# Attention a: outputs and the next keys' and values' parts one round later, the keys' rotation in two parts, weight codes converted in four passes

## The chip, the core and the metric

The kernel runs on one NeuronCore of one Trainium2 chip. A core has five engines that run their own instruction streams and meet only at semaphores: TensorE (PE; its weight loads are listed apart as PEld), VectorE (DVE), ScalarE (ACT), GpSimd (POOL) and SyncE (SP), which here issues the DMAs. Work that is being multiplied or accumulated sits in PSUM, everything else in SBUF. The metric is the device time of one execution in microseconds; smaller is better. Three runs of the kernel before took 1109.16, 1109.80 and 1110.39 us, median 1109.8 us.

## The reference, cut to what matters

The program is four layers on x of shape (2, 512, 512), each added to x after a layer norm: attention a, a mixture of low-rank experts, attention b, and the experts again. All the changed lines are in attention a:

```python
def _dequant(codes, scales):                       # codes 0..15, one scale per 128 rows and column
    return (codes.astype(jnp.float32) - 8.0) * jnp.repeat(scales, 128, axis=0)

q = h @ _dequant(q_codes, q_scales)                # h (2, 512, 512), q: 32 heads of 128
k = h @ _dequant(k_codes, k_scales)                # 8 heads of 128
v = h @ _dequant(v_codes, v_scales)
q, k = _rope(q), _rope(k)                          # pairs turned by position
k, v = jnp.repeat(k, 4, axis=1), jnp.repeat(v, 4, axis=1)
scores = jnp.einsum('bhqd,bhkd->bhqk', q, k) * 128**-0.5 + causal_mask
out = jnp.einsum('bhqk,bhkd->bhqd', jax.nn.softmax(scores), v)
return out.reshape(2, 512, 4096) @ _dequant(o_codes, o_scales)
```

## The kernel before

**Tiles.** Attention a is 64 units: 8 key heads g, 2 batches b, and 4 query heads h of each key head. A unit is one 128-wide head over 512 positions. Activations are kept transposed (head dimension on the partitions, positions along the free side) and are split into a high and a low part in a reduced-precision fp32 type, xh and xl, so that a projection is two matmuls of 128 x 512 into one PSUM bank. The scale of a group of 128 rows can only be applied to a finished 128-row product, so each projection is four products c = 0..3, each of a high and a low matmul (L358, L359). Product 0 is taken out of PSUM by ACT (L363), products 1 to 3 are multiplied by their scale and added by DVE (L365).

**The stages of a unit.** `rotated` projects and turns a query or key head: four products, two DVE multiplies of 64 partitions that swap the halves (L374, L375), then a POOL multiply and a POOL add (L376, L377). `softmaxed` makes four score tiles of 128, 256, 384 and 512 columns (i = 0..3): matmul (L396), a DVE reduction that adds the mask and finds the maximum (L399), ACT exponential (L404), after every second tile a DVE reciprocal (L411) and two POOL multiplies (L413). `weighted` transposes the probabilities on PE (L424), copies them out on ACT (L425), multiplies them by v in eight short matmuls (`av`, L429), and splits the result into ah (ACT, L151) and al (DVE, L152). `output` multiplies ah and al by the head's part of the output weight, n = 0..3 (L438, L439); product 0 goes through ACT into `part` (L445) and POOL adds it to the accumulator (L446), products 1 to 3 are multiplied and added by DVE (L448). `keys_values` projects the next key head's keys and values for both batches; values are transposed on PE (L385).

**Periods and rounds.** The loop over n starts one unit per period and runs five stages of different units side by side: `weighted` of unit n-3, `rotated` of unit n, `output` of unit n-4, `softmaxed` of unit n-2, and some parts of `keys_values`. The stages are generators; `in_turn` takes one step from each in that order, which makes a round. So in round i the program lists: the transposes of tile i, query product i, output product i, score tile i, and one key or value product. A tile scheduler then orders each engine's instructions: the earlier an instruction is in the program, the higher its priority, and an instruction that the scheduler believes not to be ready is passed by a later one. The engines run the resulting order strictly, each instruction waiting at the head of its engine's queue. In the order that results, PE places query product i behind the transposes of tile i and, where the output's operands are there in time, the two matmuls of output product i next to each other.

**Buffers that matter.** PSUM has eight banks: two each for projections (`ps_mm`), outputs (`ps_o`), scores (`ps_sc`), and transposes together with `av` (`ps_tp`). So query product c waits for the evacuation of the product two before it, and output product n for that of product n-2.

**Weights.** Codes arrive by DMA as 128 x 2048 int32 tiles; ACT subtracts 8 and writes the fp32 weight in one instruction (L317), 18 times in all: query and output weights of each g, and the second half of the key and value weights. POOL converts the first half of the key and value weights.

```python
            turn.append(some(more, 3 + (units[min(n, 63)][0] == 0)))
```

This line gives the key and value work three steps per period, four in the first eight periods. From n = 60 on, the first expert layer of batch 0 (`early`) begins beside the last units; what follows attention a is the same code before and after.

Of the kernel before, what the change touches and what calls it, by code (L numbers as in the profile page):

```python
# [14 lines left out]
AF = mybir.ActivationFunctionType  # L15
# [7 lines left out]
NC = DM // P  # L23
# [4 lines left out]
U = 512  # L28
# [12 lines left out]
def kernel(  # L41
# [21 lines left out]
    nc = tc.nc  # L63
# [216 lines left out]
    with ExitStack() as actx:  # L280
# [27 lines left out]
        def whole(codes, u, what, pool=wpool, gpsimd=False):  # L308

            cd = big.tile([P, NC * U], I32, tag="big", name=f"codes_{what}_{u}")  # L310
            nc.sync.dma_start(cd, codes[u])
            w = pool.tile([P, NC, U], F32R, tag="w", name=f"w_{what}_{u}")
            wf = w.rearrange("p c n -> p (c n)")
            if gpsimd:
                nc.gpsimd.tensor_scalar(wf, cd, -8.0, 1.0, ALU.add, ALU.mult)
            else:
                nc.scalar.activation(wf, cd, AF.Copy, bias=-8.0)  # L317
            return w

        wkv, xh, xl, own = {}, {}, {}, {}  # L320
# [2 lines left out]

        own["k"] = own_scales(k_scales, 2 * 4 * NC, "k")
        wkv["k"] = whole(k_codes, 0, "k", wkvp, gpsimd=True)
        own["q"] = own_scales(q_scales, 8 * 4 * NC, "q")
        wq = {0: whole(q_codes, 0, "q")}
        load_x("a", 1, ptp, "pT")

# [12 lines left out]
        nc.sync.dma_start(tab, rope_a)  # L342
        own["v"] = own_scales(v_scales, 2 * 4 * NC, "v")
        wkv["v"] = whole(v_codes, 0, "v", wkvp, gpsimd=True)
        two_parts(1)

# [6 lines left out]
        def projected(kind, w, u, h, b, nm):  # L353

            r = rp.tile([P, S], F32, tag=f"r{kind}", name=f"r_{nm}")
            for c in range(NC):
                ps = ps_mm.tile([P, S], F32, tag="mm", name=f"ps_{nm}_{c}")
                nc.tensor.matmul(ps, w[:, c, ts(h, A_HD)], xh[b][:, c, :], start=True, stop=False)  # L358
                nc.tensor.matmul(ps, w[:, c, ts(h, A_HD)], xl[b][:, c, :], start=False, stop=True)  # L359
                n = (u * NC + c) * 4 + h  # L360
                s = own[kind][:, n : n + 1]
                if c == 0:
                    nc.scalar.activation(r, ps, AF.Copy, scale=s)  # L363
                else:
                    nc.vector.scalar_tensor_tensor(r, ps, s, r, ALU.mult, ALU.add)  # L365
                yield
            return r

        def rotated(dst, kind, w, u, h, b, nm):


            r = yield from projected(kind, w, u, h, b, nm)
            rs = rp.tile([P, S], F32, tag=f"rs{kind}", name=f"rs_{nm}")
            nc.vector.tensor_tensor(rs[0:64], r[64:128], tab[64:128, 1, :], ALU.mult)  # L374
            nc.vector.tensor_tensor(rs[64:128], r[0:64], tab[0:64, 1, :], ALU.mult)  # L375
            nc.gpsimd.tensor_tensor(r, r, tab[:, 0, :], ALU.mult)  # L376
            nc.gpsimd.tensor_tensor(dst, r, rs, ALU.add)  # L377
            yield
# [54 lines left out]
            yield  # L433

        def output(w, h, head, b, ah, al, nm):
            for n in range(NC):
                ps = ps_o.tile([P, S], F32, tag="o", name=f"ps_o_{nm}_{n}")
                nc.tensor.matmul(ps, w[:, h, ts(n, P)], ah, start=True, stop=False)  # L438
                nc.tensor.matmul(ps, w[:, h, ts(n, P)], al, start=False, stop=True)  # L439
                s, to = so[:, head * NC + n : head * NC + n + 1], acc[b][:, n, :]  # L440
                if head == 0:
                    nc.scalar.activation(to, ps, AF.Copy, scale=s)
                elif n == 0:
                    part = rp.tile([P, S], F32, tag="part", name=f"part_{nm}")
                    nc.scalar.activation(part, ps, AF.Copy, scale=s)  # L445
                    nc.gpsimd.tensor_tensor(to, to, part, ALU.add)  # L446
                else:
                    nc.vector.scalar_tensor_tensor(to, ps, s, to, ALU.mult, ALU.add)  # L448
                yield

        def in_turn(*stages):
            stages = list(stages)
            while stages:
                stages = [st for st in stages if next(st, stages) is not stages]
# [21 lines left out]
        def keys_values(g):  # L476

            u, h = divmod(g, 4)
            if g == 4:
                wkv["k"] = whole(k_codes, u, "k", wkvp)  # L480
                wkv["v"] = whole(v_codes, u, "v", wkvp)
            for b in range(B):
                kTs[g, b] = kvp.tile([P, S], F32, tag="kT", name=f"kT_{g}_{b}")
                vs[g, b] = kvp.tile([P, NT, P], F32, tag="v", name=f"v_{g}_{b}")
                yield from rotated(kTs[g, b], "k", wkv["k"], u, h, b, f"k_{g}_{b}")
                yield from values_of(vs[g, b], wkv["v"], u, h, b, f"v_{g}_{b}")

        def chain(*stages):
            for stage in stages:
                yield from stage  # L490

        def some(stage, n):
            for _ in range(n):
                next(stage, None)
                yield


        more = keys_values(0)
        in_turn(some(more, 5))
        units = [(g, b, h) for g in range(A_NKV) for b in range(B) for h in range(A_G)]  # L500
        wo, qTs, prs, ats = {}, {}, {}, {}
        for n in range(len(units) + 4):
# [13 lines left out]
            if at(0):  # L516
                g, b, h, nm = at(0)
                if (b, h) == (0, 0):
                    if g:
                        wq[g] = whole(q_codes, g, "q")  # L520
                    wo[g] = whole(o_codes, g, "o")
                    after = keys_values(g + 1) if g + 1 < A_NKV else iter(())
                    more = chain(more, after)
                qTs[g, b, h] = qtp.tile([P, S], F32, tag="qT", name=f"qT_{nm}")
                turn.append(rotated(qTs[g, b, h], "q", wq[g], g, h, b, f"q_{nm}"))
            if at(4):
                g, b, h, nm = at(4)
                turn.append(output(wo[g], h, g * A_G + h, b, *ats.pop((g, b, h)), nm))
            if at(2):
                g, b, h, nm = at(2)  # L530
                prs[g, b, h] = []
                turn.append(softmaxed(prs[g, b, h], qTs.pop((g, b, h)), kTs[g, b], nm))
            turn.append(some(more, 3 + (units[min(n, 63)][0] == 0)))
            if n == 60:

# [531 lines left out]
```

## Time and profile before

| | |
|---|---|
| median of three runs | 1109.8 us |
| the profiled execution's own time | 1109.65 us |
| its span | 1107.9 us |
| PE busy | 1058.2 us, 96% |
| PE weight loads busy | 709.3 us, 64% |
| DVE busy | 862.7 us, 78% |
| ACT busy | 616.9 us, 56% |
| POOL busy | 586.3 us, 53% |
| first `av` matmul of attention a | 60.3 us |
| weight conversion on ACT, 128 x 2048 | 1.91 us each, 18 of them |

The span is cut into 40 slices on the page; attention a fills the first 25 of them, up to about 700 us. A group of instructions is given with its busy time, the mean duration of one, and the idle time of its engine just before it with what ended that idle time. Matmuls are pipelined: a matmul's duration covers its weight's wait and its latency, so that two neighbours overlap and PE looks busy even where the next one starts late. The distance from the start of one matmul to the start of the next, read in the timeline, shows that; it is called the pitch below.

### The profile page before, as it was taken

The numbers are of one execution on the slowest core, as the hardware profiler recorded it, in microseconds if no ns is written. First come the engines' busy times: TensorE is split into PE (matmuls) and PEld (weight loads), VectorE is DVE, ScalarE is ACT, GpSimd is POOL, SyncE is SP. The second block draws the span as 40 slices with busy tenths as digits, with TensorE's granted clock in tenths as the row PEclk, the third lists the DMA queues.
The fourth block names the chain that finished last, engine by engine and source line by source line (L and its number), as shares of the span: only waits on it lengthen the run. The fifth ranks groups of instructions, "written<-read, shape, count | busy, mean of one in ns | idle before, by whom it ended". The sixth has DMA issues, their size and how long they took to land.

```text
span 1107.9 us, 16182 instructions
## 1 busy us (share of the span) xinstructions
PE 1058.2 (96%) x4940; PEld 709.3 (64%) x4940; DVE 862.7 (78%) x2175; ACT 616.9 (56%) x1421; POOL 586.3 (53%) x916
## 2 busy tenths in 40 slices
PE   4799999999999999999999999999989999999988
PEld 3467777777777677777677777556457555565534
DVE  6889899999999999999999888665386677766142
ACT  3566665566656656665666666523156577675410
POOL 2466556656656556566666666353235576544200
PEclk9899999999999999999999999999999999989999
DMA  7300010121110110110112000023352235211010
GB/s 290 114 1 32 8 39 1 39 76 39 38 39 1 39 39 1 38 39 1 39 45 70 1 1 1 1 94 91 99 178 57 80 107 165 90 39 45 18 48 38
DMA packets 23270, 60.47 MB, mean 55 GB/s; under 512 B 4368, under 2 KB 5328, under 8 KB 20368
## 3 DMA queue, kind: packets, MB, share of 16 engines
q1 hardware_dynamic: 23184, 59.44, 16.4%
q8 instruction: 40, 0.66, 0.2%
q14 instruction: 46, 0.38, 0.1%
HBM read 45.53 MB, written 12.85 MB: 53 GB/s over the span
## 4 chain that ended last, share of the span: by engine, by line
PE 83%; DVE 6%; DMA 3%; POOL 3%; ACT 2%; issue 2%; SPq 0%; ACTq 0%; DVEq 0%; POOLq 0%
PE av L429 12%; PE sc L396 12%; PE tp L424 6%; PE ps_o L438 5%; PE ps_o L439 5%; PE ps_q L358 5%; PE ps_q L359 5%; PE ph_f L207 5%; PE py_f L266 4%; PE num_b L831 3%; PE st_b L805 3%; PE sc_b L758 3%; PE po L887 2%; PE pq_b L678 2%; DMA spread_q<-hl 1%
## 5 line engine op out<-in xcount | busy, mean ns | idle before, releaser
L404 ACT ACTIVATE p<-sc,nmx 128x128 f32<-128x128 f32 (+3 forms) x256 | 135.5, 529 | 95.6 <-DVE nmx L399 92.7
L376 POOL TENSOR_TENSOR r_q<-r_q,tab 128x512 f32<-128x512 f32 x64 | 82.4, 1287 | 191.4 <-DVE rs_q L375 191.4
L396 PE MATMUL sc<-kT,qT 128*128 128x128 f32 (+3 forms) x512 | 180.2, 433 | 0.7 <-POOL qT L377 0.7
L365 DVE SCALAR_TENSOR_TENSOR r_q<-ps_q,s_q,r_q 128x512 f32<-128x512 f32 x192 | 143.6, 748 | 37.2 <-PE ps_q L359 23.3
L413 POOL TENSOR_SCALAR p<-p,rden 128x128 f32<-128x128 f32 (+3 forms) x256 | 139.6, 558 | 59.2 <-DVE rden L411 20.5
L425 ACT COPY pT<-tp 128x128 f32<-128x128 f32 (+3 forms) x256 | 109.3, 427 | 104.3 <-PE tp L424 103.6
L762 DVE CUSTOM_DVE_ANT_0 sc_b<-sc_b,tri 128x128 f32<-128x128 f32 (+3 forms) x256 | 119.7, 517 | 49.5 <-PE sc_b L758 40.4
L429 PE MATMUL av<-pT,v 128*128 128x512 f32 (+3 forms) x512 | 148.5, 433 | 0.0
L429 PEld LDWEIGHTS av<-pT,v 128*128 128x128 f32 x512 | 97.0, 190 | 80.2 <-issue 53.9
L448 DVE SCALAR_TENSOR_TENSOR acc<-ps_o,s_o,acc 128x512 f32<-128x512 f32 x186 | 137.5, 739 | 5.5 <-PE ps_o L439 5.4
L399 DVE CUSTOM_DVE_ANT_0 sc<-sc,tri 128x128 f32<-128x128 f32 (+3 forms) x256 | 125.4, 490 | 7.9 <-PE sc L396 7.0
L358 PE MATMUL ps_q<-xh,w_q 128*128 128x512 f32 x256 | 123.8, 483 | 7.8 <-DVE r_q L365 7.8
L424 PE MATMUL tp<-ident,p 128*128 128x128 f32 x640 | 112.9, 272 | 2.4 <-POOL p L413 2.4
L396 PEld LDWEIGHTS sc<-kT,qT 128*128 128x128 f32 x512 | 95.9, 189 | 24.7 <-ACT p L404 1.5
L811 ACT ACTIVATE pT_b<-st_b 128x384 f32<-128x384 f32 (+1 forms) x192 | 90.5, 528 | 35.6 <-PE st_b L805 34.4
L438 PE MATMUL ps_o<-ah,w_o 128*128 128x512 f32 x256 | 108.0, 422 | 1.7 <-DVE acc L448 1.0
L439 PE MATMUL ps_o<-al,w_o 128*128 128x512 f32 x256 | 104.8, 410 | 3.5 <-DVE al L152 3.5
L424 PEld LDWEIGHTS tp<-ident,p 128*128 128x128 f32 x640 | 82.9, 141 | 30.4 <-issue 6.4
L359 PE MATMUL ps_q<-xl,w_q 128*128 128x512 f32 x256 | 102.2, 399 | 0.0
L814 POOL TENSOR_SCALAR_AFFINE_SELECT pT_b<-pT_b 128x128 f32<-128x128 f32 (+1 forms) x192 | 63.0, 338 | 65.2 <-ACT pT_b L811 62.0
L377 POOL TENSOR_TENSOR qT<-r_q,rs_q 128x512 f32<-128x512 f32 x64 | 85.3, 1334 | 1.0
L446 POOL TENSOR_TENSOR acc<-acc,part 128x512 f32<-128x512 f32 x62 | 79.7, 1285 | 10.1 <-ACT part L445 10.1
(179 smaller groups left out, 2042.5 us busy)
## 6 DMA issues: line engine op xcount, KB each, us to landing
codes_q<-in_q_codes_dram SPq DMA_DIRECT2D x8, 1024.0 KB
codes_o<-in_o_codes_dram SPq DMA_DIRECT2D x8, 1024.0 KB
spread_q<-hl SPq DMA_DIRECT2D x16, 512.0 KB
qs<-spread_q SPq DMA_DIRECT2D x32, 256.0 KB
x_a<-in_x_dram SPq DMA_DIRECT2D x8, 256.0 KB
codes_k<-in_k_codes_dram SPq DMA_DIRECT2D x2, 1024.0 KB
codes_v<-in_v_codes_dram SPq DMA_DIRECT2D x2, 1024.0 KB
x_r<-in_x_dram SPq DMA_DIRECT2D x8, 256.0 KB
```

The lines of the kernel that those rows point to most:

```text
L358: nc.tensor.matmul(ps, w[:, c, ts(h, A_HD)], xh[b][:, c, :], start=True, stop=False)
L359: nc.tensor.matmul(ps, w[:, c, ts(h, A_HD)], xl[b][:, c, :], start=False, stop=True)
L365: nc.vector.scalar_tensor_tensor(r, ps, s, r, ALU.mult, ALU.add)
L396: nc.tensor.matmul(sc[:, :n], qT[:, ts(i, P)], kT[:, :n], start=True, stop=True)
L399: nc.vector.tensor_tensor_reduce(sc[:, :n], sc[:, :n], tri[:, S - n :], -(A_HD**-0.5), 3e38, ALU.add, ALU.min, nmx,)
L404: nc.scalar.activation(pr, sc[:, :n], AF.Exp, bias=nmx, scale=-1.0, accum_out=den[:, i % 2 : i % 2 + 1],)
L413: nc.gpsimd.tensor_scalar(prs[j], prs[j], rden[:, j % 2 : j % 2 + 1], 1.0, ALU.mult, ALU.mult)
L424: nc.tensor.transpose(tp[:, j, :], prs[i][:, ts(j, P)], ident)
L429: nc.tensor.matmul(av[:, j * P :], v[:, j, :], pT[:, j, j * P :], start=(j == 0), stop=(j == NT - 1))
L438: nc.tensor.matmul(ps, w[:, h, ts(n, P)], ah, start=True, stop=False)
L439: nc.tensor.matmul(ps, w[:, h, ts(n, P)], al, start=False, stop=True)
L448: nc.vector.scalar_tensor_tensor(to, ps, s, to, ALU.mult, ALU.add)
```

## The change

Four edits, all in attention a:

- `output` begins with a bare step, so its product n stands in round n+1; the last one falls in a round of its own, with the key and value parts.
- `some` begins with a bare step as well, so the key and value parts take rounds 1 to 3 (1 to 4 in the first eight periods) where they took rounds 0 to 2 (0 to 3). The call ahead of the loop takes six steps in place of five.
- In `rotated`, keys (not queries) get a step between the two DVE multiplies that swap the halves. A key head now has six steps instead of five.
- The conversion of codes on ACT is four instructions of 128 x 512 in place of one of 128 x 2048.

```diff
             else:
-                nc.scalar.activation(wf, cd, AF.Copy, bias=-8.0)
+                for c in range(NC):
+                    nc.scalar.activation(wf[:, ts(c, U)], cd[:, ts(c, U)], AF.Copy, bias=-8.0)
             return w
...
             nc.vector.tensor_tensor(rs[0:64], r[64:128], tab[64:128, 1, :], ALU.mult)
+            if kind == "k":
+                yield
             nc.vector.tensor_tensor(rs[64:128], r[0:64], tab[0:64, 1, :], ALU.mult)
...
         def output(w, h, head, b, ah, al, nm):
+
+            yield
             for n in range(NC):
...
         def some(stage, n):
+            yield
             for _ in range(n):
                 next(stage, None)
                 yield
...
         more = keys_values(0)
-        in_turn(some(more, 5))
+        in_turn(some(more, 6))
```

No matmul, transfer or buffer is added or taken away. ACT has 54 more instructions (72 conversions in place of 18). The order of the instructions that SP issues is the same as before; on PE, DVE, ACT and POOL the order changes throughout attention a and is the same again from the norm of the first expert layer on batch 1 on.

## The prediction

> **What bounds the kernel now.** I read the page first, then busy time by stage, then the chain that ended last, then the waits of PE, then the timeline of two periods. The page shows PE full through the whole of attention a, which is the first 25 slices, and DVE nearly so:
>
> ```profile
> span 1107.9 us, 16182 instructions
> PE 1058.2 (96%) x4940; PEld 709.3 (64%) x4940; DVE 862.7 (78%) x2175; ACT 616.9 (56%) x1421; POOL 586.3 (53%) x916
> PE   4799999999999999999999999999989999999988
> DVE  6889899999999999999999888665386677766142
> ```
>
> Busy time in three stretches, each cut where an `av` begins (columns: length, then busy time of PE, PEld, DVE, ACT, POOL, granted clock, DMA share, GB/s): eight periods with key and value work, the next four, and eight without it.
>
> ```profile
> 488.65:572.98 84.33, 83.30 (x377) 60.78 (x376) 77.38 (x169) 51.57 (x129) 52.61 (x60) 1.00 0.08 26
> 572.98:614.01 41.03, 40.70 (x185) 29.64 (x184) 38.14 (x84) 24.94 (x63) 26.27 (x30) 1.00 0.24 78
> 614.01:688.94 74.93, 74.93 (x338) 54.47 (x337) 65.44 (x153) 45.87 (x120) 46.47 (x56) 1.00 0.00 1
> ```
>
> PE is busy 74.93 of 74.93 us, and yet not at its pace. In the timeline a matmul over 512 columns is followed by the next after 0.23 us, a transpose after 0.108, and the score and `av` matmuls come as two records each, 0.108, 0.215, 0.322 and 0.428 apart by width. A unit without keys and values has 16 wide matmuls, 10 transposes and eight record pairs: 3.68 + 1.08 + 2 x 2.146 = 9.05 us. It takes 74.93/8 = 9.37. Adding 0.23 for each key or value matmul and 0.43 for a transposed value tile, I set each `av`-to-`av` distance against its own contents. From 60.3 to 698.4 us, 61 periods take 638.1 us for 609.0 us of pitches: 29.1 us are hidden waits. The starts in the chain show where they lie:
>
> ```profile
> 488.81 2.16 PE av L429 x8
> 499.09 2.16 PE av L429 x8
> 510.40 2.16 PE av L429 x8
> 520.52 2.16 PE av L429 x8
> 529.84 2.16 PE av L429 x8
> 540.60 2.16 PE av L429 x8
> 548.08 1.07 DVE rs_k L375
> 551.82 2.16 PE av L429 x8
> ```
>
> By these contents most periods lose 0.17 to 0.32 us, the one from 499.09 loses 0.89, the one from 540.60 loses 1.25. The waits that PE and its weight loads show from 60 to 700 us name the two causes, and the timeline the events:
>
> ```profile
> PEld ps_o L439 <- DVE al L152: 9.1, 20, 1.8
> PEld ps_q L358 <- DVE r_q L365: 7.2, 7, 1.0
> ```
>
> ```profile
> 501.59 1.13 DVE L374 TENSOR_TENSOR rs_q<-r_q,tab 64x512 f32<-64x512 f32 x1
> 502.75 0.69 DVE L152 TENSOR_TENSOR al<-av,ah 128x512 fp32r<-128x512 f32 x1
> 503.50 0.19 PEld L439 LDWEIGHTS ps_o<-al,w_o 128*128 128x128 f32 x1 [0.76 <-DVE al L152]
> ...
> 549.18 0.75 DVE L365 SCALAR_TENSOR_TENSOR r_q<-ps_q,s_q,r_q 128x512 f32<-128x512 f32 x1
> 549.99 0.50 PE L358 MATMUL ps_q<-xh,w_q 128*128 128x512 f32 x1 [0.70 <-DVE r_q L365]
> ```
>
> Output product 0 asks for ah and al right after `av`, too early. And the second half of a key's swap stands in DVE's queue ahead of the evacuation `r_q` that frees query product 3's bank. So attention a is bound by PE with DVE's queue biting into it; ACT (51.57 of 84.33) and POOL have room.
>
> **The change part by part.** The sum is made against the profiled execution, 1109.65 us (span 1107.9 and 1.75 around it), 0.15 under the median.
>
> *Outputs a round later.* The built order of PE shows it: output product 3 now stands behind the next `av`, product 0 behind query product 1, and high and low matmuls stand together nearly everywhere, where before about two of them per period were parted by other work. Where the pattern is whole today (from 675.45 to 679.57 us) half a period costs 4.12 us for 4.096 of pitches. So the floor of a period is its pitches + 0.045: 61 x 0.045 = 2.7 us. What is late next is al. In 44 of the units DVE's order is now acc of output 3, then al. From the start of `av`: 2.15 + 0.46 of output 3, whose low matmul is out 0.39 after its start, at 2.77; DVE sees it 0.04 later; acc 0.74, al 0.69 from 0.08 before acc's end: 4.16; PE sees it at 4.21. Its weight load would like 4.07, and a late one puts the next matmul 0.34 behind it (549.99 to 550.33), at 4.55 where it would be at 4.53: 44 x 0.03 = 1.3 us. Both ends: zero, and 0.3 if DVE is not free at 2.8.
>
> *Key and value parts a round later.* Same matmuls; they stand behind score tiles 1 to 3, their DVE evacuations a whole round ahead of the bank's next use. In a period with three parts DVE then runs without a gap from query product 2 to al; adding its rows (0.75, 0.74, reductions 0.57 to 0.75 with their read, swaps 0.69 with 0.03 before each) al reaches PE 0.26 after its wish instead of 0.14, and the next matmul stands 0.14 late: some four per group of eight, 27 in all, 3.9 us (0 to 0.3 each). Behind the first `av`, three parts and a value transpose more than before now fall into full periods, 1.8 us; the start, with PE busy 40.16 of 60.29 us, loses the same work. I take zero, with 1.5 either way.
>
> *Keys' swap in two parts.* The second half no longer blocks query product 3. But the halves count still: in one period per group both halves and an evacuation land where no key matmul lengthens PE's side (DVE 10.3 against 9.5 us), al is late by 0.56 there; in one more, a half stands right ahead of al beside POOL's multiply: 0.4. 6 x 0.56 + 7 x 0.4 = 6.2 us. Both ends: zero if the queue has slack, 1.07 each (the slow row at 548.08). A swap runs without overlap on both sides: at 671.19 it starts 0.03 after the operation before has ended, while at 673.84 a reduction starts 0.08 before al ends. Parting two halves thus costs DVE 0.13; by the built order 7 key pairs and 23 query pairs more are parted: 3.9 us of DVE, contained in the lateness above. The Trainium skill speaks against the change here: "VectorE: DVE Perf Modes", section on two Vector instructions with no wait between them, says that an instruction whose input or output starts in another group of 32 partitions than the one before starts only when all earlier ones are finished. The trace agrees (0.03 after, against 0.08 before the end); the sum by the rule is the one above.
>
> *Four passes.* ACT pays for 54 more starts. A 128x512 copy takes 0.586 (L425) and a scaled one 0.704 (L363), so four take 2.3 to 2.8 against 1.91: 18 x 0.4 to 0.9 = 8 to 16 us of ACT, which has 40% free in these periods. On the path: the weight of output 3 is read a period later, so its buffer's next conversion moves behind ah, and one pass of about 0.59 stands ahead of the first transposes' copy, which the next transposes wait for: 0.3 in each of six periods, 1.8 us (0 to 0.7 each). Nothing gained at the start, where the query weight is ready long before its first matmul. SP's order is unchanged.
>
> Left in the 61 periods: 2.7 + 1.3 + 3.9 + 6.2 + 1.8 = 15.9 of 29.1 us. The change gives 13.2 us: 1109.65 - 13.2 = 1096.5. What follows 700 us keeps its order.
>
> **The rivals.**
> 1. *All the lateness is absorbed.* Only floor and al remain, 4.0 us: 1084.6. For: six of eight periods already hide DVE's peaks behind other matmuls today. Against: the new order has nothing left that PE could take while it waits.
> 2. *PE is full already, or DVE takes over.* If DVE keeps its 6.95 us idle per group, groups with keys and values stay at 84.3 and only nine periods without them gain 0.24: 1107.5; half of that gives 1104. For: DVE 77.38 of 84.33 and 3.9 more. Against: DVE's idle time there is mostly waiting for ah and for query products, which PE's pace sets. That PE looks full is no support: the Trainium skill, "Perfetto Trace Analysis", section "Identifying the Most-Contended Engine", calls matmul busy a bad measure and takes the weight loads' instead; they are at 73% in the third stretch, which would promise a quarter, while the pitches here leave 3.4%, so the measurement decides.
> 3. *Slower.* al behind acc is the one new wait in the order. If DVE reaches acc of output 3 late in every period, because the swaps ahead of it run beside POOL's additions (1.13 for 0.69 at 501.59), PE stands at output product 0 with nothing to pass. From 0.30 us more in each of 44 periods the gain is gone; at 0.44, that row's excess, it is 1109.65 - 13.2 + 19.4 = 1115.8. Against: POOL's multiply waits for both swaps, so it begins behind them.
> 4. *It does nothing:* excluded for PE's order, which is seen in the built program.
>
> **How the numbers follow.** Forecast 0.60 (1090 to 1102), rival 1 0.16 (to 1084), rival 2 0.14 (1102 to 1108), rival 3 0.10. A measurement here tells a change from none at about 0.2%, 2.2 us. Faster: 0.60 + 0.16 + 0.12 = 0.88; within: 0.04; slower: 0.08. The range 1086 to 1106 leaves out half of rival 1 (0.07), the end of rival 2 (0.03) and rival 3.
>
> **What would show it.** Right: periods without keys and values at 9.1 to 9.2 us between `av` starts; the period of 11.2 down to about 10.1 with less key work in it; PE's wait for al by its longest under 0.8; the 62nd `av` beginning near 685 us instead of 698; ACT's conversions at 0.55 to 0.7 each. Wrong: periods of 9.37 or more without keys, or a PE wait for al in nearly every period of over 0.3; a later part that changes though its order is the same.

## Result and profile after

The changed kernel takes 1102.53 us (median of 4 runs, 1101.25 to 1104.38), the kernel before beside it 1109.48 (1108.8 to 1110.39): a ratio of 0.9935, 95% interval 0.992 to 0.9951. The profiled execution is of 1102.45 us with a span of 1100.7, 7.2 us under that of before. The page, span and busy times first, then the slices of PE and DVE:

```profile
span 1100.7 us, 16226 instructions
PE 1048.4 (95%) x4940; PEld 701.4 (64%) x4940; DVE 872.1 (79%) x2175; ACT 626.9 (57%) x1475; POOL 601.9 (55%) x916
PE   4799999999999999999999999999989989999988
DVE  6889899999999999999999999665386667776142
```

DVE is busy 9.4 us longer than before and POOL 15.6, though both have the same number of instructions: some of them have become slower. The same three stretches of attention a as before the change, each cut where an `av` begins (length, then busy time of PE, PEld, DVE, ACT, POOL, granted clock, DMA share, GB/s):

```profile
482.15:566.05 83.90, 82.64 (x377) 59.97 (x376) 78.59 (x169) 52.73 (x134) 55.31 (x60) 1.00 0.08 26
566.05:607.39 41.34, 40.94 (x187) 29.58 (x186) 38.84 (x84) 26.55 (x67) 27.65 (x30) 1.00 0.24 77
607.39:680.47 73.08, 73.08 (x337) 53.14 (x336) 67.36 (x153) 46.27 (x120) 46.55 (x56) 1.00 0.00 1
```

Eight periods without keys and values went from 74.93 to 73.08: 9.135 each where the pitches are 9.05. Eight periods with them went only from 84.33 to 83.90, for the same matmuls. Setting every `av`-to-`av` distance against the pitches of its contents, as the prediction did, the 61 periods now hold 22.9 us of lateness, and held 29.1. Of the 6.2 us gained 2.7 lie in the first eight periods, 1.85 in the eight without keys and values, and only 1.9 in the 44 between; the 61st loses 0.3. The first `av` begins at 55.46 instead of 60.29 with 2.9 us of matmuls fewer ahead of it (1.8 of keys and values, the rest of score tiles), which is 1.9 us net. These 1.9 us need not be the change's. In the profile before, the clock granted to TensorE was about half from 49.6 to 53.1 us, where its wide matmuls follow one another after 0.43 instead of 0.23 us; after the change there is no such stretch from 35.5 us to the first `av` (length, then the columns as above: before, then after):

```profile
49.60:53.10 3.50, 3.50 (x11) 2.37 (x10) 3.05 (x8) 2.02 (x6) 2.21 (x2) 0.51 0.00 0
35.50:55.46 19.96, 15.39 (x62) 9.20 (x61) 16.93 (x35) 12.20 (x27) 10.65 (x10) 1.00 0.27 107
```

PE is busy for the whole 3.5 us, so by an estimate the stretch costs up to 1.7 us, half of its length. So the 62nd `av` begins 8.2 us earlier, at 690.16. What follows takes 410.6 us, and 409.6 before. Of this 1.0 us 0.46 is an output product (two matmuls) that now stands behind the 62nd `av`; in the runs below it takes 409.7 to 415.7, so the rest can't be told from no change.

What is late in the 44 periods is seen in the waits of PE and its weight loads from 60 to 690 us (total, times, longest):

```profile
PEld ps_o L444 <- DVE al L152: 19.2, 45, 1.5
PE ps_o L444 <- DVE al L152: 7.3, 11, 1.1
PEld ps_q L359 <- DVE r_q L366: 1.4, 3, 0.6
```

The wait for `r_q` is nearly gone (7.2 us in 7 waits before). The wait for `al` has grown from 9.1 us in 20 to 19.2 in 45, the longest 1.5 where it was 1.8. The chain that ended last shows what stands ahead of the longest, in the period from 543.65, which is 1.48 us over its pitches:

```profile
545.31 0.70 DVE rs_k L378
546.01 0.02 issue
546.03 0.69 DVE rs_q L375
...
546.94 1.03 DVE rs_q L378
547.98 0.47 issue
548.45 0.70 DVE al L152
549.15 0.04 issue
549.19 0.50 PE ps_o L444
```

The second half of the query's swap begins at 546.94 and al only at 548.45, 1.51 us later: the half takes 1.47 us instead of 0.69. It starts inside POOL's multiply of the key, which had waited for the key's own two halves and began right behind them, at 546.08:

```profile
546.08 1.79 POOL L379 TENSOR_TENSOR r_k<-r_k,tab 128x512 f32<-128x512 f32 x1 [3.49 <-DVE rs_k L378]
546.94 1.47 DVE L378 TENSOR_TENSOR rs_q<-r_q,tab 64x512 f32<-64x512 f32 x1
```

In the timeline of another period, from 502.74 and 0.755 over its pitches, the partner is POOL's addition of the key:

```profile
502.26 1.28 POOL L379 TENSOR_TENSOR r_k<-r_k,tab 128x512 f32<-128x512 f32 x1
503.62 1.27 POOL L380 TENSOR_TENSOR kT<-r_k,rs_k 128x512 f32<-128x512 f32 x1
504.07 1.36 DVE L375 TENSOR_TENSOR rs_q<-r_q,tab 64x512 f32<-64x512 f32 x1
505.45 0.69 DVE L378 TENSOR_TENSOR rs_q<-r_q,tab 64x512 f32<-64x512 f32 x1
...
506.89 0.68 DVE L152 TENSOR_TENSOR al<-av,ah 128x512 fp32r<-128x512 f32 x1
```

POOL's addition of the key ends at 504.89; the swap that started inside it ends at 505.43, 0.54 us later; then acc of output 3 and al follow without a gap. Of the 61 periods five are about 1.47 over their pitches, and nine with key and value work stand between 0.70 and 0.84: behind the first eight, each group of eight with that work has one of the first kind and one or two of the second. That named the theory to test (P): *DVE has no slack ahead of al, and the swaps that meet an operation of POOL are what makes al late*. The rivals: the load of DVE alone (D), and the parting of the swap's halves itself (S).

### The profile page after: what moved, and what is told of

The parts are those of the page before. It is cut to its first block, busy times and chain, and to the rows that moved or that the text cites. A ratio compares the mean times of both kernels' runs of the same rounds, so it can differ in the third digit from the quotient of the medians.

```text
span 1100.7 us, 16226 instructions
## 1 busy us (share of the span) xinstructions
PE 1048.4 (95%) x4940; PEld 701.4 (64%) x4940; DVE 872.1 (79%) x2175; ACT 626.9 (57%) x1475; POOL 601.9 (55%) x916
## 4 chain that ended last, share of the span: by engine, by line
PE 70%; DVE 19%; issue 3%; ACT 3%; DMA 3%; POOL 2%; SPq 0%; DVEq 0%; ACTq 0%; POOLq 0%
PE sc L399 9%; PE av L432 9%; PE tp L427 5%; PE ph_f L207 5%; PE ps_o L444 4%; PE ps_q L359 4%; PE ps_q L360 4%; PE ps_o L443 4%; DVE r_q L366 3%; PE st_b L811 3%; PE num_b L837 3%; PE sc_b L764 3%; PE po L893 2%; PE pq_b L684 2%; DVE acc L453 2%
## 5 line engine op out<-in xcount | busy, mean ns | idle before, releaser
L416 POOL TENSOR_SCALAR p<-p,rden 128x128 f32<-128x128 f32 (+3 forms) x256 | 151.9, 606 | 123.5 <-DVE rden L414 102.6
L407 ACT ACTIVATE p<-sc,nmx 128x128 f32<-128x128 f32 (+3 forms) x256 | 135.7, 530 | 86.6 <-DVE nmx L402 84.3
L399 PEld LDWEIGHTS sc<-kT,qT 128*128 128x128 f32 x512 | 95.7, 189 | 21.9 <-ACT p L407 2.0
L427 PEld LDWEIGHTS tp<-ident,p 128*128 128x128 f32 x640 | 78.6, 140 | 30.1 <-issue 8.2
L451 POOL TENSOR_TENSOR acc<-acc,part 128x512 f32<-128x512 f32 x62 | 80.7, 1302 | 13.2 <-ACT part L450 13.2
L380 POOL TENSOR_TENSOR qT<-r_q,rs_q 128x512 f32<-128x512 f32 x64 | 82.5, 1289 | 2.8
```

What stands on the lines that cost most here:

```text
L399: nc.tensor.matmul(sc[:, :n], qT[:, ts(i, P)], kT[:, :n], start=True, stop=True)
L407: nc.scalar.activation(pr, sc[:, :n], AF.Exp, bias=nmx, scale=-1.0, accum_out=den[:, i % 2 : i % 2 + 1],)
L416: nc.gpsimd.tensor_scalar(prs[j], prs[j], rden[:, j % 2 : j % 2 + 1], 1.0, ALU.mult, ALU.mult)
L427: nc.tensor.transpose(tp[:, j, :], prs[i][:, ts(j, P)], ident)
```

## Experiments

Times on different chips differ by 0.2% and more (before: 1107.5 to 1110.0 in these batches), so each kernel stands by its ratio to the kernel before on the same chip, and by where its 62nd `av` begins in its profile, which leaves out what comes behind attention a. That place contains the start, though, and before the first `av` these profiles have between none and 10.3 us at about half the granted clock, which need not be the kernel's doing. The lateness in the 61 periods does not contain the start and is the safer measure (only "one step less ahead" has such a stretch inside them, 3.4 us from 53.8). "Stuck" counts DVE's swaps of over 1.0 us, of some 148 from 60 to 690 us (132 to 134 where POOL does half of a key's).

| kernel | ratio, 95% interval | 62nd av | lateness in 61 periods | stuck |
|---|---|---|---|---|
| before | 1 | 698.4 | 29.1 | 15 |
| changed | 0.9935, 0.992 to 0.9951 | 690.2 | 22.9 | 14 |
| outputs later alone | 1.0041, 1.0023 to 1.0058 | 698.4 | 30.5 | 15 |
| keys and values later alone | 1.0068, 1.0053 to 1.0083 | 704.6 | 33.2 | 17 |
| changed, swap whole | 0.998, 0.9968 to 0.9992 | 693.0 | 26.6 | 15 |
| changed, one pass | 0.9967, 0.9954 to 0.9981 | 692.6 | 25.2 | 17 |
| changed, keys and values not later | 1.0045, 1.0027 to 1.0064 | 700.2 | 31.6 | 21 |
| changed, keys' POOL work later | 0.9894, 0.9874 to 0.9915 | 686.2 | 19.9 | 15 |
| changed, keys not rotated | 0.986, 0.9842 to 0.9878 | 681.4 | 15.5 | 4 |
| changed, step behind the swap | 0.9933, 0.9914 to 0.9951 | 687.8 | 20.9 | 13 |
| POOL work later, half on POOL | 0.9925, 0.991 to 0.994 | 685.5 | 21.9 | 15 |
| the same, one step less ahead | 0.9945, 0.9928 to 0.9963 | 689.5 | 24.1 | 15 |
| the same, one step more ahead | 1.0047, 1.0032 to 1.0062 | 699.1 | 31.8 | 26 |
| POOL work and value transposes later | 0.9934, 0.9913 to 0.9956 | 689.0 | 21.1 | 16 |

### Each part alone, or left out

The outputs alone, on the kernel before:

```
         def output(w, h, head, b, ah, al, nm):
+            yield
```

> The kernel before with one edit: the outputs enter a period a round later. The account by terms: the wait of output product 0 for ah and al, about 0.30 us over the pitches in some 45 ordinary periods, falls to the 0.09 that the changed kernel shows in its ordinary periods; 45 x 0.21 = 9.5 us, so about 1100 us. The periods in which a key's swap stands in DVE's queue (1.25 and 0.89 over the pitches) stay over 0.7. Rival, the gain of the changed kernel came from the keys' and values' parts instead: within 2 us of 1109.5, ordinary periods still at 9.36.

It became slower: the 62nd `av` begins where it did, and the lateness rose by 1.4 us. The ordinary periods did fall to 9.12 us, as the account said. But the periods with keys and values rose: two of eight to about 1.1 and 1.55 over the pitches, from 0.89 and 1.25, and most of the others stayed near 0.3. PE's waits (60 to 690 us) show that the wait for `al` was exchanged for one that the outputs had covered:

```profile
PEld ps_q L358 <- DVE r_q L365: 14.1, 17, 1.3
PE ps_q L358 <- DVE r_q L365: 9.7, 12, 1.0
...
PEld ps_o L440 <- DVE al L152: 3.0, 15, 0.8
```

In the period from 541.67 a half of the key's swap starts inside POOL's addition of output 0, takes 1.66 us, and the evacuation of `r_q` that frees the bank stands behind it. The keys and values alone:

```
         def some(stage, n):
+            yield
             for _ in range(n):
...
-        in_turn(some(more, 5))
+        in_turn(some(more, 6))
```

> The kernel before with one edit: the keys' and values' parts enter a period a round later. The account by terms: PE's wait for r_q (7 waits over 0.7 us, up to 1.0) is mostly gone, worth 3 to 6 us, but the swaps now stand ahead of al, which is still asked for too early, and 2 to 4 us come back; 1105 to 1109, ordinary periods still at 9.36. Rival, this edit carries the gain: 1103 or less.

Slower than either number. The ordinary periods stayed at 9.34 to 9.37, as expected, but one period in eight went to 1.65 over the pitches: a query's swap of 1.68 us, stuck in POOL's key multiply, ahead of an al that is asked for right behind `av`. So neither edit has a gain of its own. By the lateness, the two edits added up would have cost 1.4 + 4.1 = 5.5 us; together, with the four passes, they gain 2.5. That is the next run, the changed kernel with the key's swap whole:

```
             nc.vector.tensor_tensor(rs[0:64], r[64:128], tab[64:128, 1, :], ALU.mult)
-            if kind == "k":
-                yield
```

> The changed kernel with the keys' swap in one part again. Theory P, the long periods (1.47 and 0.75 over the pitches) come from DVE's swaps running beside POOL's multiply and addition of the keys: the key's addition still falls beside a query's swap, so the time is within 3 us of 1102.5 and rows of swaps over 1.0 us remain. Rival S, the parting of the two halves is the cost: about 10 us less, 1093, with no period over 10.9. Rival Q, the parting is what keeps a whole swap out of the way of query product 3: the wait for r_q comes back, 1107 or more.

At the pace of the first chip, 0.998 is 1107 us: Q by the time. By the rows both hold: PE's wait for `r_q` is back at 2.8 us in 6 (0.7 in 2 with the parting), and 15 swaps are stuck, one of 1.68 us ahead of al in each period of 1.8 over the pitches. S falls: without the parting nothing is gained. Parting is worth 2.9 us up to the 62nd `av`, and 3.7 us of lateness.

The changed kernel with the codes converted in one pass:

```
-                for c in range(NC):
-                    nc.scalar.activation(wf[:, ts(c, U)], cd[:, ts(c, U)], AF.Copy, bias=-8.0)
+                nc.scalar.activation(wf, cd, AF.Copy, bias=-8.0)
```

> The changed kernel with the codes converted in one pass again. The account by terms: one pass of 1.91 us stands on ACT where one of about 0.6 stands now, ahead of the copy of the first transposes, so the periods with the output weight's conversion, 0.29 over the pitches now, go to about 1.5, in six periods: 1102.5 + 7 = 1109. Rival, the conversion is covered and the starts of four passes are all that the edit costs: 1101 to 1102.5, those periods at 0.1 to 0.3.

Between the two. The periods with the output weight's conversion are at 0.32 to 0.37, not at 1.5, though the pass of 1.92 us stands where the one of 0.64 stood, between ah and the first transposes' copy (486.30 here, 485.04 in the changed kernel). So my account of that pass was wrong; the four passes are worth 2.4 us up to the 62nd `av` another way. In the three groups behind 404 us the two periods that follow a conversion changed from 0.35 and 0.75 over the pitches to 0.10 and 1.53, which is 1.6 of the 2.4; in the second a query's swap of 1.14 us stands in POOL's key addition, and PE waits for transposes and for al in turn. Why one pass leads to that place was not traced. (This kernel's profiled execution, 1108.0, is 4 us over its median; behind attention a it takes 413.7 us.)

The changed kernel with the keys and values not later:

```
         def some(stage, n):
-            yield
...
-        in_turn(some(more, 6))
+        in_turn(some(more, 5))
```

> The changed kernel with the keys' and values' parts entering in the first round of a period, as before: what the later round is worth when the outputs are late as well. By the sum of the parts (outputs alone gave nothing in attention a, the swap in two parts 2.9 us, four passes 2.4 us): 1104. By my account of terms, in which the later round frees the bank of query product 3: 1106 to 1108. Rival, the later round costs here too, as it does alone (6 us): 1096 to 1098.

All three expectations were missed: 1.0045 is about 1114 at the first chip's pace. Taking this edit away from the changed kernel costs 10 us up to the 62nd `av` (8.7 of lateness); adding it to the kernel before cost 6 (4.1 of lateness). In this order 21 swaps are stuck, 9 of the key's in POOL's addition of output 0, at 1.57 us each on the mean.

### POOL's key work moved, or taken away

One step more for the keys, so that POOL's two operations enter a round after the swap:

```
             nc.vector.tensor_tensor(rs[64:128], r[0:64], tab[0:64, 1, :], ALU.mult)
+            if kind == "k":
+                yield
             nc.gpsimd.tensor_tensor(r, r, tab[:, 0, :], ALU.mult)
```

> The changed kernel with one more step for the keys: POOL's multiply and addition of a key's rotation enter a round after the second half of its swap. In POOL's order they then follow output 0's addition, at the start of a period, where DVE's reductions run, and no longer stand next to a swap. Theory P, the periods of 1.47 and 0.75 over the pitches come from swaps beside POOL's key operations: the swaps of 1.2 to 1.5 us are gone, those periods fall to 0.1 to 0.4, and of the 12.8 us that they cost (5 x 1.38 and 9 x 0.66) 8 to 11 go: 1092 to 1095. Rival D, the load of DVE in the periods with a key's evacuations is the cause, whatever POOL does: the swaps get short, but long periods stay, 1100 to 1104.

It beats both kernels: 0.9894, with an interval that lies below the changed kernel's. Of the 12.9 us that the long periods cost, 3 in all went, less than P said. The periods of 1.47 are gone, but now the same period of every four stands at 0.79, and the timeline says why:

```profile
530.94 1.29 POOL L381 TENSOR_TENSOR r_q<-r_q,tab 128x512 f32<-128x512 f32 x1
532.31 1.27 POOL L382 TENSOR_TENSOR qT<-r_q,rs_q 128x512 f32<-128x512 f32 x1
532.53 1.59 DVE L378 TENSOR_TENSOR rs_k<-r_k,tab 64x512 f32<-64x512 f32 x1
533.54 1.74 POOL L453 TENSOR_TENSOR acc<-acc,part 128x512 f32<-128x512 f32 x1
```

The key's second half now starts 0.22 us inside the query's addition and again ends 0.54 behind its end (533.58 to 534.12). Everything behind it on DVE is late up to the next al. P's mechanism held; that no swap would meet another operation of POOL was wrong.

Taking POOL's key work away altogether:

```
-            nc.gpsimd.tensor_tensor(r, r, tab[:, 0, :], ALU.mult)
-            nc.gpsimd.tensor_tensor(dst, r, rs, ALU.add)
+            if kind == "k":
+                nc.scalar.copy(dst, r)
+            else:
+                nc.gpsimd.tensor_tensor(r, r, tab[:, 0, :], ALU.mult)
+                nc.gpsimd.tensor_tensor(dst, r, rs, ALU.add)
```

> The changed kernel in which the keys are not rotated: ACT copies the key product where POOL multiplied and added, so the scores are those of keys without rotation; DVE's swaps of the keys still run, for nothing. Theory P: no swap over 0.9 us is left, no period over 0.4 above its pitches, 1090 to 1094. Rival D, DVE's load alone: swaps get short, periods of 0.7 to 1.5 stay, 1100 to 1104. In between, 1095 to 1100: the swaps' own queueing is part of it.

0.986, or 1094 at the first chip's pace: the end of P's range, though not all of its rows came: four swaps of 1.04 to 1.78 us are left, and periods of 0.66 to 0.81. The query's swaps (by line: min, median, max in ns; the 60 to 61 of each half from 60 to 690 us), in the changed kernel:

```profile
L375 DVE TENSOR_TENSOR rs_q<-r_q,tab x61: 683/687/1369, 59.7 to 681.5; 64x512 f32<-64x512 f32 x61
L378 DVE TENSOR_TENSOR rs_q<-r_q,tab x61: 684/685/1472, 60.6 to 682.2; 64x512 f32<-64x512 f32 x61
```

and without POOL's key work, none over 0.69:

```profile
L375 DVE TENSOR_TENSOR rs_q<-r_q,tab x60: 683/687/690, 66.4 to 672.5; 64x512 f32<-64x512 f32 x60
L378 DVE TENSOR_TENSOR rs_q<-r_q,tab x60: 684/685/689, 68.5 to 673.2; 64x512 f32<-64x512 f32 x60
```

Period by period the two causes part: in five of the nine periods of 0.70 to 0.84 the lateness falls to 0.10, so there the stuck swap was all of it. The five of 1.47 fall to between 0.66 and 0.74: about 0.8 was the stuck swap, and the 0.6 that stays fits DVE's load, as D says: in that run DVE works from 537.08 to the end of al at 540.90 with no gap over 0.03 us, a half of a key's swap and both of a query's among it. Together 7.3 of the 12.9 us of the long periods go with POOL's key work, and the lateness as a whole falls by 7.4. The 0.35 of the period from 492.87 stays.

The other four of the nine keep their 0.70 to 0.81. In three of them (in the changed kernel from 101.74, 217.85 and 334.39) the swap that is stuck is the *key's*, in POOL's addition of the *query*, which this run left in place. It stands ahead of the evacuation that frees a query product's bank (changed kernel):

```profile
340.05 1.28 POOL L380 TENSOR_TENSOR qT<-r_q,rs_q 128x512 f32<-128x512 f32 x1
340.27 1.60 DVE L378 TENSOR_TENSOR rs_k<-r_k,tab 64x512 f32<-64x512 f32 x1
341.91 0.75 DVE L366 SCALAR_TENSOR_TENSOR r_q<-ps_q,s_q,r_q 128x512 f32<-128x512 f32 x1
342.71 0.50 PE L359 MATMUL ps_q<-xh,w_q 128*128 128x512 f32 x1 [0.35 <-DVE r_q L366]
```

In the fourth, from 78.80, no swap is stuck; its cause was not traced.

The step moved from between the halves to behind both:

```
-            if kind == "k":
-                yield
             nc.vector.tensor_tensor(rs[64:128], r[0:64], tab[0:64, 1, :], ALU.mult)
+            if kind == "k":
+                yield
             nc.gpsimd.tensor_tensor(r, r, tab[:, 0, :], ALU.mult)
```

> The changed kernel with the keys' extra step moved: not between the two halves of the swap, but behind both, ahead of POOL's multiply. In POOL's order the first key of a group still has its multiply and addition right ahead of a query's, the second has them at the start of a period. Theory P: one of the two kinds of long period goes and the other stays: 1096 to 1100. Rival S, parting the halves is what costs: both go, 1090 to 1094. Rival Q, a whole swap ahead of query product 3 costs as much as before: 1104 or more.

0.9933 is the changed kernel's ratio, 1102 at the first chip's pace, between the numbers of P and Q. S falls for good: parting the halves is not what costs. By the periods from 400 us on, one kind went from 0.75 to 0.49 and the other from 1.47 to 1.10, with a query's swap of 1.13 still in the latter; none of them went altogether, as P had said of one kind.

### Half of the key's swap on POOL

These three build on the kernel with the keys' POOL work a round later. They take 0.69 us per key off DVE and give it to POOL, and differ by the round in which the keys' steps fall. They set the place of a swap against the load of DVE.

```
+            half = nc.gpsimd if kind == "k" else nc.vector
-            nc.vector.tensor_tensor(rs[64:128], r[0:64], tab[0:64, 1, :], ALU.mult)
+            half.tensor_tensor(rs[64:128], r[0:64], tab[0:64, 1, :], ALU.mult)
```

> The kernel with the keys' POOL work a round later, and the second half of the key's swap on POOL instead of DVE. Rule under test (from the rows so far): a swap on DVE that starts inside a two-input operation of POOL ends about 0.69 us after that operation's end, while one that is already running when POOL's starts keeps its 0.69 and lengthens POOL's. DVE loses the 12 swaps of 1.6 us; but POOL now does three operations (3.9 us) behind a period's first two normalisations, 1.7 us ahead of an av, and they end 2.2 to 2.5 us behind it, across the query's swaps (1.3 to 2.7 us behind it): one period in four keeps 0.6 to 0.8 over its pitches, 1096 to 1098. If it is DVE's load and not the place, the 0.69 less on DVE shows: 1090 to 1092.

One period in four stands at 0.87 to 0.96 over its pitches (forecast 0.6 to 0.8), with a query's swap of 1.47 in POOL's key multiply; nearly all others are at 0.09 to 0.29. The time, 1101 at the first chip's pace, is outside both numbers, further from that of the load than from that of the place. The rule's 0.69 us behind POOL's end was too long: in all rows so far it is 0.54 to 0.56. With one step less ahead of the first unit:

```
-        in_turn(some(more, 6))
+        in_turn(some(more, 5))
```

> As the kernel before it, with one step less ahead of the first unit, which moves the keys' steps by a round in every period. In POOL's order the half swap stands ahead of the later two normalisations, the key's multiply behind the query's, the addition behind the query's addition: none of them beside a query's swap. By the rule no swap over 0.9 us is left and every period of the steady part is under 0.4 over its pitches: 8 to 9 us less than the kernel with the keys' POOL work a round later, 1089 to 1091. Rival, the load of DVE ahead of al (here a key's evacuation, both halves of a query's swap and one of a key's stand in a row): one period in four keeps 0.6 or more, 1096 or more.

Missed: one period in four at 1.10 to 1.12. I had placed POOL's half swap behind the first two normalisations at once; it waited 3.96 us for the key's last evacuation and, in the period that I followed, ran at 530.10. The query's second half started inside it and took 1.46, and the key's first half, behind that, took 0.96 inside a normalisation. These two excesses, 0.77 and 0.27, are the whole 1.02 over the floor. The rival got its number, not its reason. And with one step more than the first of the three:

```
-        in_turn(some(more, 6))
+        in_turn(some(more, 7))
```

> As the same kernel with one step more ahead of the first unit. DVE's order is the lightest of the three (the key's half swap stands ahead of query product 3's evacuation, nothing of a key's ahead of al), but POOL does the key's multiply and addition right ahead of the query's multiply, across the query's swaps. By the rule one period in four keeps 0.6 to 0.8, 1096 to 1098, worse than with one step less; by DVE's load it is the best of the three, 1089 to 1091.

DVE's lightest order of the three is slower than the kernel before, so D alone can't be the cause; but the rule under-priced it, one period in four being at 1.77 to 1.98 over its pitches. The timeline of one of them:

```profile
536.95 1.27 POOL L382 TENSOR_TENSOR r_k<-r_k,tab 128x512 f32<-128x512 f32 x1
538.29 1.29 POOL L383 TENSOR_TENSOR kT<-r_k,rs_k 128x512 f32<-128x512 f32 x1
...
538.42 1.71 DVE L375 TENSOR_TENSOR rs_q<-r_q,tab 64x512 f32<-64x512 f32 x1
...
540.14 0.68 DVE L379 TENSOR_TENSOR rs_q<-r_q,tab 64x512 f32<-64x512 f32 x1
...
541.58 0.68 DVE L152 TENSOR_TENSOR al<-av,ah 128x512 fp32r<-128x512 f32 x1
...
542.32 0.50 PE L447 MATMUL ps_o<-al,w_o 128*128 128x512 f32 x1 [1.23 <-DVE al L152]
```

The swap starts 0.13 us inside the key's addition (ends 539.58) and ends 0.55 behind it; nothing on DVE has slack up to al, and PE stands 1.23 us.

### The load ahead of a stuck swap

The last question was whether the 0.79 of the kernel with the keys' POOL work a round later is the sum of a stuck swap and of DVE's load before it. Here, on that kernel, a value's transposes wait for three products of the next key, so that one evacuation less stands in the period ahead:

```
+        late = [iter(())]
...
-                yield from rotated(kTs[g, b], "k", wkv["k"], u, h, b, f"k_{g}_{b}")
-                yield from values_of(vs[g, b], wkv["v"], u, h, b, f"v_{g}_{b}")
+                key = rotated(kTs[g, b], "k", wkv["k"], u, h, b, f"k_{g}_{b}")
+                value = values_of(vs[g, b], wkv["v"], u, h, b, f"v_{g}_{b}")
+                for part in (key, key, key, late.pop(), key, key, key, key, value, value, value, value):
+                    next(part, None)
+                    yield
+                late.append(value)
...
-        in_turn(some(more, 6))
+        in_turn(some(more, 7))
```

> The kernel with the keys' POOL work a round later, in which the transposes of a value's tile wait until three products of the next key are out, and one step more stands ahead of the first unit. DVE's and POOL's orders around the swaps stay: the second half of a key's swap still starts inside the query's addition and takes 1.6 us, and al of the following unit is 0.79 over the pitches late. What changes is DVE's load before it: in the period ahead, one key evacuation instead of two, and on PE the transposes beside it. Theory, lateness adds up over two periods where DVE has more to do than PE: PE less DVE by rows was -0.5 and -0.55 in these two periods and is now +0.1 and -0.55, so the 0.79 falls to about 0.3, in 12 periods, 5 to 6 us: 1091 to 1094. Rival, the 1.6 us swap alone sets it, whatever stands before: 0.79 stays, 1097 to 1099.

The rival was right: those periods stand at 0.79 to 0.84, as before, and the swaps at 1.6. Load that DVE has worked off before the stuck swap leaves nothing behind. The time is worse than either number, and the difference lies at the start: the first `av` begins at 55.9 instead of 53.6, and the first period is 0.95 us later. How much of that is the edit is open, since in this profile 10.3 us before the first `av` ran at half the granted clock, and 6.9 in the other.

## Why the prediction was right, and where it was off

The direction was right. The time, 1102.5, lies in the whole range, but just past the end of the forecast's own (1090 to 1102), where rival 2's began; the gain was 7.2 us of the 13.2 forecast. In the 61 periods, where all 13.2 were to come from, it was 6.2: 22.9 us of lateness were left and not 15.9. The start, which the sum had at zero, gave the 1.9 that bring the total nearer, and what follows lost 1.0. As up to 1.7 of the start's gain is the granted clock of the two profiles, that part is luck.

- *Outputs a round later; key and value parts a round later.* Floor, al behind acc of output 3 and the three-part periods were priced at 2.7 + 1.3 + 3.9 = 7.9 us. The runs show 0.07 to 0.12 over the pitches in periods with none of the other causes, three-part ones among them: 61 x 0.09 = 5.5. The forecast of 9.1 to 9.2 for ordinary periods held (9.12 to 9.16). But this gain belongs to the two edits together, which the prediction did not say: each alone made the kernel slower.
- *Keys' swap in two parts.* This is the term that was mis-sized: 6 x 0.56 + 7 x 0.4 = 6.2 us. The periods priced at 0.56 (as from 492.87) stand at about 0.35, eight in all, 2.1 us over their floor. Those priced at 0.4, with a half of a key's swap right ahead of al beside POOL's multiply (as from 543.65), stand at 1.47, five of them, and nine of about 0.75 had no term of their own: 5 x 1.39 + 9 x 0.66 = 12.9 us. The second half no longer blocks a query product in the steady groups, as said, but it still does in the periods from 217.85 and 334.39. The price was off since I bounded the lengthening by the 1.07 of one row, and let a half "beside POOL's multiply" cost 0.4; a half that starts early in a POOL operation of 1.29 us takes up to 1.8 (1.785 is the longest in this profile). The profile before already held one of 1.68, at 73.74, which would have given a wider bound. That I let rival 3 go with "POOL's multiply waits for both swaps, so it begins behind them" is the failing step: it waits for the *key's* two halves, and what meets it are the *query's*, which come right behind in DVE's queue.
- *Rival 2.* In the steady groups with keys and values it was nearly right: 84.33 to 83.90 where it said 84.3. Its reason was not: DVE did not keep its 6.95 us idle per group (83.90 - 78.59 = 5.3 are left), and without POOL's key work the same eight periods take 82.45.
- *Four passes.* The lateness of 0.3 in six periods came (0.28 to 0.30, of which 1.2 us over the floor against 1.8 forecast), but the length of the pass ahead of the copy, the reason given, does not set it: a pass three times as long in the same place leaves these periods at 0.32 to 0.37. The passes take 0.62 to 0.68 us, as forecast. That they gain something was not foreseen; it is 2.4 us up to the 62nd `av`, most of it in periods behind the conversions.
- *Startup.* Taken as zero with 1.5 either way: 1.9 us gained net, up to 1.7 of them by the stretch at half the granted clock that only the profile before has.
- *What would show it.* The period of 11.2 (from 540.44 before) went below 10.1, to 9.61 with half of its key work (from 534.04 after); its lateness did not go but moved to the next one, 11.91 from 543.65. The wait for al was not under 0.8 (1.1 on PE), and the 62nd `av` began at 690 and not at 685. These two, and the 11.91, come from the mis-sized term.

## What to carry to other kernels

Before moving work on one engine's queue, lay the other engine's queue beside it: an elementwise operation with two inputs in SBUF on DVE must not start while POOL is inside an operation, and which pair meets is decided by a few tenths of a us. In a software pipeline an edit of the order has no value of its own: two edits that each lost 0.4 to 0.7% were part of a gain, so test them together and then each one left out. Where two engines have no slack, price an edit by the longest wait that the new neighbours allow, not by the one row that the old order happened to show.

## What was not expected of the hardware

How exactly the two engines exclude one another. In the traces of all fourteen kernels, from 60 to 690 us, every swap that starts at least 0.3 us before the end of one of POOL's multiplies or additions of two tiles ends 0.54 to 0.56 us behind that operation's end (224 rows, swaps of 0.86 to 1.79 us), and no swap that starts outside an operation of POOL takes over 0.70. Where POOL's operation starts inside a running swap, the swap keeps its 0.68 to 0.69 and POOL's becomes longer: in the changed kernel the key's multiply takes 1.78 to 1.79 us instead of 1.28 in the five periods of 1.47, and a normalisation of 384 columns 1.0 instead of 0.59. al, whose other input comes from PSUM, is untouched: at 0.68 us inside the query's multiply of 1.29 (506.89 in the changed kernel). The Trainium skill states this rule on the page "SBUF — State Buffer", section "Who interferes with whom": a Vector instruction with two SBUF inputs contends with a GpSimd instruction that reads SBUF, and the order of issue decides which of them blocks. The traces agree. They add the size: the blocked swap is out 0.54 us after POOL's end, less than its own 0.69.
